# MLP rows of batches 4 and 5 turned by VectorE and SBUF transfers instead of TensorE, in a PixArt block on one Trainium2 core

## The chip, the cores and the metric

The kernel runs on one core of one Trainium2 chip. The core has a TensorE for matrix products (PE in the profile), a VectorE (DVE), a ScalarE (ACT), a GpSimd (POOL) and a SyncE (SP, which here only issues transfers). Each engine works through its own queue of instructions in order and waits on semaphores that the others set. All compute engines read and write an on-chip memory, the SBUF; matrix products end in a second one, the PSUM. The metric is the device time of one execution in microseconds (us). Before the change the median of three runs is 738.39 us (736.37, 740.21 and 738.39).

## The reference

One transformer block over 16 batches of 256 rows of 256 features, all float32: modulated self-attention, cross-attention to a context, and a modulated MLP. The change touches the MLP and the passage from attention to it.

```python
shift_a, scale_a, gate_a, shift_m, scale_m, gate_m = jnp.split(silu(c) @ W_mod + b_mod, 6, axis=-1)
...
x = x + c_attn_out                                   # end of cross-attention
x_norm2 = modulate(_ln(x), shift_m, scale_m)         # t * (1 + scale) + shift, per batch
h = gelu(x_norm2 @ W_mlp1 + b_mlp1)                  # 256 -> 1024
h = h @ W_mlp2 + b_mlp2                              # 1024 -> 256
x = x + gate_m[:, None] * h
```

## The kernel before, in words

Attention comes first. Thirty-two units (16 of self-attention, 16 of cross-attention) run in eight beats each; a plan says which pieces stand in each beat. The result of a batch's cross-attention, `t_c`, goes to DRAM (`x2d`). In the last units, words of a table named `TW` are dealt into the beats: `u0` to `u7` load the MLP weights, `h..` and `l..` split each weight into a high part and the rest (a product of float32 rows is made of three products of such parts, `mm3`), `x2` loads the rows of batch 2, `b2` adds the constant `cb` to them. A letter at the end names the engine: `d` VectorE, `p` or none GpSimd.

The MLP of a batch `b` is a chain of steps, each on its engine:

- `x`: load the rows from `x2d` (SP). `b`: add `cb` (GpSimd). `s`: statistics (VectorE: BN_STATS, BN_AGGR). `p`: the power that gives one over the deviation (GpSimd, `rs_m`). `a`: normalise (VectorE, `xn_m`).
- The rows must then stand with features on partitions. `mlp_T` (L833) has TensorE turn them (four transposes into `psT_m`), and VectorE and ScalarE scale, shift and split them into `hi` and `lo`. These two parts live in old weight tiles: `wkch` and `wkcl` for even batches, `wqch` and `wqcl` for odd ones.
- `mlp_turn` (L857) does it without TensorE: VectorE turns blocks of 32 by 32 (`z`), and four SBUF transfers issued by SP move the blocks to their partitions (`yT`). `mlp_turned` (L870) then scales and shifts on VectorE (two `z<-yT`), copies `hi` and subtracts to get `lo`. The rows of a turned batch come out in another order, and the GELU's writing puts it right by its access pattern (L931), at the cost of no further instruction.
- `F` j: first product, quarter j % 4 of batch j // 4, twelve TensorE products into `ph`. `G` j: two GELUs on ScalarE (`hf` in float32, `hh` rounded), then `hl` = `hf` - `hh` on GpSimd, written hl(j) below. `S` j: the twelve second products, which read `hh` and `hl`, into `st` (even batches) or `s` (odd ones). After a batch's last `S`, VectorE multiplies by the gate (`mt`) and adds the residual (`y`), and SP stores. `r` prepares that residual (`xmg`), `g` loads the gates (`gm`).

`TURN` (L855) says from which batch on the turned path is taken: 6 before. The passage from attention to MLP is written out as a string of words, `BE`; it reaches to the middle of batch 3 (F13 and S10). From then on a loop deals the rest. In it, one step is one quarter j; the loop issues G of j+1, F of j+2, S of j-1, and at fixed quarters the steps of the batches ahead:

```python
by_dma = [d if d < B and d >= TURN else None for d in range(b + 1, b + 4)]
by_pe = b + 2 if b + 2 < TURN else None
```

Batches in `by_dma` are loaded, biased and measured three batches ahead, and normalised and turned two ahead; the one in `by_pe` is prepared two ahead and turned by TensorE one ahead. Program order on every engine is the order in which these words are issued; nothing reorders them. A tile with a fixed number of buffers holds its next writer back until the last reader of the oldest buffer is done; `hh` and `hl` have three buffers each, so the GELU of j into `hh` waits for S of j-3.

Of the kernel before, what the change touches and what calls it, by code (L numbers as in the profile page):

```python
# [16 lines left out]
P = 128  # L17
# [4 lines left out]
def pixart_block(  # L22
# [85 lines left out]
    brow = const.tile([32, P], F32, name="brow")  # L108
# [151 lines left out]
    wm = []  # L260
# [9 lines left out]
    gm = []  # L270
# [19 lines left out]
    def layernorm(src, name):  # L290
# [542 lines left out]
    def mlp_T(b):  # L833
# [9 lines left out]
        for f in range(KC):  # L843
            DVE.tensor_scalar(y[:, f], pst[:, f * N:(f + 1) * N], sc1[:, 1, f, b:b + 1],
                              cpT[:, 6 + f, b:b + 1], ALU.mult, ALU.add)
        if b in E_['DV']:
            DVE.tensor_copy(hi, y)
# [4 lines left out]
        DVE.tensor_tensor(lo, y, hi, ALU.subtract)  # L852
        m.xT = (hi, lo)

    TURN = 6  # L855

    def mlp_turn(b):  # L857

# [23 lines left out]
    NCH = NF // 2  # L882

    def mlp_first(b, c):

        ph = ps_gen(f"ph_{b}_{c}", LONG).rearrange("p (j n) -> p j n", j=2)
        for j in range(2):
            mm3(ph[:, j], W1, 2 * c + j, M[b].xT)
        M[b].h[c] = ph
# [27 lines left out]
    def mlp_gelu(b, c):  # L917
# [6 lines left out]
        for dst in (hf, hh):  # L924
# [13 lines left out]
    def mlp_second(b, c):  # L938
# [15 lines left out]
        if done and b < B - 1:  # L954
            for t in range(NT):
# [7 lines left out]
    wf = {}  # L963

    steps = {"x": mlp_load, "b": mlp_bias, "s": mlp_stats, "p": lambda b: M[b].ln.pow(), "a": mlp_apply,
             "r": mlp_residual, "g": mlp_gates, "T": mlp_T, "F": lambda j: mlp_first(j // NCH, j % NCH),
             "G": lambda j: mlp_gelu(j // NCH, j % NCH), "S": lambda j: mlp_second(j // NCH, j % NCH)}

    def tail_word(w):
# [26 lines left out]
    u0, u1 = units[:2]  # L996
# [4 lines left out]
    u2 = units[2]  # L1001
# [42 lines left out]
    u3 = units[3]  # L1044
# [182 lines left out]
    last, o, q = units[-1], units[-1].post, units[-2].post  # L1227
# [97 lines left out]
```

## Time and profile before

| | |
|---|---|
| median of three runs | 738.39 us (736.37 to 740.21) |
| the profiled execution: its time | 737.4 us |
| its span, first to last instruction | 735.6 us |
| TensorE busy | 728.9 us (99%) |
| VectorE busy | 584.8 us (79%) |
| ScalarE busy | 555.5 us (76%) |
| GpSimd busy | 546.3 us (74%) |
| granted TensorE clock | 0.999 |

A row of a timeline gives the start in us from the span's beginning, the duration, the engine, the line, the operation, what is written and from what, its size, how many instructions were merged (their common span is the duration), and in brackets the idle time ahead of it with what ended that. Every operation goes through one recording helper, so all rows carry line 51; they are told apart by their tiles. TensorE products are pipelined: each lasts 0.28 us, but they start 0.12 us apart. In a row of waits stand the time waited in all, how often, and the longest.

### The profile page before, as it was taken

The page shows a single profiled execution, that of the slowest core. Times are in us where ns is not written, and L with a number is a line of the kernel's source. Part 1 is how long each engine was busy: PE and PEld are TensorE (multiplying, and loading weights), DVE is VectorE, ACT ScalarE, POOL GpSimd, SP SyncE. Part 2 cuts the span into 40 slices and gives each one's busy share as a digit, 9 for nine tenths or more (in the row PEclk, how much of TensorE's full clock was granted, in tenths as well). Part 3 has the DMA queues.
Part 4 walks back from the last instruction along what each step waited for, and adds up shares of the span by engine and source line. Part 5 has one row for each costly group of instructions (what it writes and reads, how often), then busy time and mean ns, then how long its engine had stood idle before and what let it go on. Part 6 is the DMA issues. An engine that isn't in the chain of part 4 may idle for free.

```text
span 735.6 us, 25307 instructions
## 1 busy us (share of the span) xinstructions
PE 728.9 (99%) x10112; PEld 644.8 (88%) x10112; DVE 584.8 (79%) x1217; ACT 555.5 (76%) x959; POOL 546.3 (74%) x571
## 2 busy tenths in 40 slices
PE   9999999999999999999999999999999999999997
PEld 9878888888888888888888888888889999999997
DVE  4788898989888888988888989888735577687772
ACT  3268898888888888888888888899887655555553
POOL 6777688869687786968778798788657766767753
PEclk9999999999999999999999999999999999999999
DMA  6754454543545454454545555455312323323331
GB/s 190 205 166 142 125 142 134 141 122 101 155 114 155 125 144 137 107 152 112 160 126 139 143 156 146 126 151 140 96 60 58 102 61 98 98 90 102 87 77 38
DMA packets 94825, 90.60 MB, mean 123 GB/s; under 512 B 9266, under 2 KB 90452, under 8 KB 94708
## 3 DMA queue, kind: packets, MB, share of 16 engines
q1 hardware_dynamic: 94244, 88.20, 42.8%
q8 instruction: 80, 1.31, 0.8%
q0 software_dynamic: 192, 0.52, 0.3%
q14 instruction: 37, 0.30, 0.1%
q10 hardware_dynamic: 272, 0.26, 0.1%
HBM read 26.97 MB, written 8.46 MB: 48 GB/s over the span
## 4 chain that ended last, share of the span: by engine, by line
PE 93%; DVE 3%; POOL 2%; issue 1%; ACT 1%; DMA 1%; SPq 0%; POOLq 0%; ACTq 0%
PE s L51 18%; PE o L51 16%; PE st L51 16%; PE ph L51 10%; PE ps_q L51 5%; PE ps_qc L51 4%; PE ps_v_c L51 3%; PE ps_kc L51 3%; PE ps_P_s L51 3%; PE ps_k L51 2%; PE ps_v_s L51 2%; PE ps_P_c L51 2%; DVE mx L51 1%; PE psT_q L51 1%; PE ps_h L51 1%; PE psA_s L51 1%
## 5 line engine op out<-in xcount | busy, mean ns | idle before, releaser
L51 DVE TENSOR_REDUCE mx<-s 128x2 f32<-128x512 f32 x504 | 324.8, 684 | 64.4 <-PE s L51 57.7
L51 ACT ACTIVATE pt<-st 128x1024 f32<-128x1024 f32 x252 | 258.9, 1027 | 16.4 <-PE st L51 10.4
L51 PE MATMUL s<-big 63*128 63x256 f32 (+1 forms) x1024 | 184.0, 297 | 0.2
L51 PEld LDWEIGHTS s<-big 63*128 63x128 f32 (+1 forms) x1024 | 133.4, 186 | 18.7 <-DVE l_kc L51 6.6
L51 PE MATMUL st<-big 64*128 64x256 f32 (+1 forms) x1024 | 134.6, 298 | 0.5 <-ACT pt L51 0.2
L51 POOL TENSOR_TENSOR hl<-hf,hh 128x512 fp32r<-128x512 f32 x64 | 87.0, 1361 | 52.9 <-ACT hh L51 52.8
L51 PE MATMUL o<-pt,v 128*32 128x256 f32 x2048 | 123.8, 382 | 0.0
L51 PEld LDWEIGHTS st<-big 64*128 64x128 f32 (+1 forms) x1024 | 96.3, 186 | 16.1 <-issue 13.1
L51 PEld LDWEIGHTS o<-pt,v 128*32 128x32 f32 x2048 | 60.1, 110 | 41.4
L51 ACT ACTIVATE hf<-ph,bT 128x256 f32<-128x256 f32 x114 | 47.8, 471 | 33.1 <-PE ph L51 33.0
L51 ACT ACTIVATE hh<-ph,bT 128x256 fp32r<-128x256 f32 x114 | 47.9, 472 | 28.0 <-PE s L51 14.4
L51 ACT COPY oT<-o 128x512 f32<-128x512 f32 x63 | 36.9, 586 | 33.1 <-PE o L51 33.1
L51 PE MATMUL st<-big,hh 128*128 128x256 f32 x256 | 46.7, 282 | 0.0
L51 PE MATMUL s<-big,hh 128*128 128x256 f32 x256 | 46.7, 281 | 0.0
L51 PE MATMUL ph<-wkch,wself 128*128 128x256 f32 x224 | 44.4, 282 | 0.0
L51 PE MATMUL ph<-wqch,wself 128*128 128x256 f32 x224 | 44.3, 282 | 0.0
L51 PE MATMUL ps_k<-xTh_s,wself 64*128 64x256 f32 (+1 forms) x232 | 43.6, 294 | 0.0
L51 POOL TENSOR_SCALAR xn_c<-c,mv_c,rs_c 128x256 f32<-128x256 f32 x32 | 39.0, 1227 | 1.7
L51 PE MATMUL ps_q<-xTh_s,wself 64*128 64x256 f32 (+1 forms) x240 | 39.7, 282 | 0.0
L51 PE MATMUL ps_P_s<-wself,xTh_as 64*128 64x256 f32 x256 | 39.1, 282 | 0.0
L51 PEld LDWEIGHTS s<-big,hh 128*128 128x128 f32 x256 | 39.0, 189 | 0.0
L51 PEld LDWEIGHTS st<-big,hh 128*128 128x128 f32 x256 | 39.0, 189 | 0.0
(250 smaller groups left out, 2500.4 us busy)
## 6 DMA issues: line engine op xcount, KB each, us to landing
big<-h_kc SPq DMA_DIRECT2D x64, 128.0 KB
big<-h_qc SPq DMA_DIRECT2D x64, 128.0 KB
big<-h_k SPq DMA_DIRECT2D x62, 128.0 KB
big<-h_q SPq DMA_DIRECT2D x62, 128.0 KB
big<-l_k SPq DMA_DIRECT2D x32, 128.0 KB
big<-l_q SPq DMA_DIRECT2D x32, 128.0 KB
g<-gd SPq DMA_DIRECT2D x16, 256.0 KB
c<-in_ctx_dram SPq DMA_DIRECT2D x16, 256.0 KB
```

Of the source, the lines that this page charges most:

```text
L51: i = f(*a, **k)
```

## The change

Three edits. `TURN` goes from 6 to 4, so batches 4 and 5 take the turned path. A new word `W` (`mlp_turn`) lets the string `BE` turn batch 4, which the loop comes too late to do, and the word `T` picks the path by batch. And the words of `TW` and `BE` are dealt anew; below, the entries that differ.

```diff
-    'TW': (23, 7): 'u1', (28, 0): 'l2 h0p u5', (28, 7): 'u4 u6', (29, 2): 'l1',
-          (30, 1): 'u7 h6d h7p', (30, 3): 'h4p', (31, 2): 'l5d x2', (31, 4): 'l7', (31, 7): 'b2'
+    'TW': (24, 4): 'u1', (28, 0): 'u5 l2 h0p', (28, 7): 'u4 u6 l1',
+          (30, 1): 'u7 h6d', (30, 3): 'h4p h7p', (31, 2): 'x2', (31, 3): 'l5d', (31, 4): 'l7 b2'
...
-    'BE': 'G0 av P g0 A1 G1 G2 N1 F7 g1 S0 PF s2 G3 aT aL p2 a2 G4 x3 b3 S1 S2 T2 C r0 G5 S3 G6 S4 s3 CF x4
-           F8 g2 G7 S5 F9 p3 S6 G8 a3 r1 G9 F10 G10 T3 g3 b4 S7 s4 F11 S8 S9 F12 G11 p4 a4 F13 r2 S10 G12 x5'
+    'BE': 'g0 G0 av P A1 G1 G2 N1 F7 g1 S0 PF s2 G3 aT aL x3 p2 a2 G4 b3 S1 S2 T2 C G5 r0 S3 G6 S4 s3 CF x4
+           F8 G7 g2 S5 F9 p3 S6 G8 a3 r1 G9 F10 G10 T3 S7 g3 b4 s4 F11 S8 x5 F12 G11 p4 a4 F13 S9 W4 r2 S10 G12 b5 s5'
...
-    TURN = 6
+    TURN = 4
...
-             ... "T": mlp_T,
+             ... "T": lambda b: (mlp_turned if b >= TURN else mlp_T)(b), "W": mlp_turn,
```

TensorE loses the turns of batches 4 and 5. This is the place in front of F14 (`ph_2` of batch 3), before, with four transposes of batch 4 between the last products of S10 and F14:

```order
L51 MATMUL st<-big_77,hh_2_12554 128x256 x2
L51 MATMUL st<-big_77,hl_2_12555 128x256
L51 MATMUL psT_m_12708<-ident,xn_m_12660 128x128 x4
L51 MATMUL ph_2_12721<-wqch,wself 128x256
L51 MATMUL ph_2_12721<-wqcl,wself 128x256
```

After the change F14 follows S10 directly there, the same is so at batch 5's turn in front of F18, and S9 stands behind F12 and F13 instead of ahead of them.

VectorE, from the statistics of batch 4 to the end of its rows, before (`xTf_m` is the scaled row from `psT_m`; ScalarE writes `wkch`):

```order
L51 BN_STATS st_m_12593<-x_4_12455 128x6 x2
L51 BN_AGGR mv_m_12596<-st_m_12593 128x2 x2
L51 TENSOR_SCALAR xn_m_12660<-x_4_12455,mv_m_12596,rs_m_12599 128x256 x2
L51 TENSOR_TENSOR xmg_12676<-x_2_12076,gm_12470 128x512
L51 TENSOR_SCALAR xTf_m_12713<-psT_m_12708,sc_103,cpT 128x256 x2
L51 TENSOR_TENSOR wkcl<-xTf_m_12713,wkch 128x512
L51 TENSOR_TENSOR mt_12734<-st,gm_12470 128x256 x2
L51 TENSOR_TENSOR y_12735<-xmg_12676,mt_12734 128x512
L51 BN_STATS st_m_12788<-x_5_12698 128x6 x2
L51 BN_AGGR mv_m_12791<-st_m_12788 128x2 x2
L51 TENSOR_SCALAR xn_m_12864<-x_5_12698,mv_m_12791,rs_m_12794 128x256 x2
```

The same place after the change, up to the turn of batch 5:

```order
L51 TENSOR_SCALAR xn_m_12650<-x_4_12455,mv_m_12596,rs_m_12599 128x256 x2
L51 STREAM_TRANSPOSE z_12678<-xn_m_12650 128x2x4x32 x2
L51 TENSOR_TENSOR xmg_12686<-x_2_12075,gm_12478 128x512
L51 BN_STATS st_m_12709<-x_5_12625 128x6 x2
L51 BN_AGGR mv_m_12712<-st_m_12709 128x2 x2
L51 TENSOR_SCALAR z_12678<-yT_12679,sc_103,cpT 128x4x64 x2
L51 COPY wkch<-z_12678 128x512
L51 TENSOR_TENSOR wkcl<-z_12678,wkch 128x512
L51 TENSOR_TENSOR mt_12745<-st,gm_12478 128x256 x2
L51 TENSOR_TENSOR y_12746<-xmg_12686,mt_12745 128x512
L51 TENSOR_SCALAR xn_m_12796<-x_5_12625,mv_m_12712,rs_m_12715 128x256 x2
L51 STREAM_TRANSPOSE z_12799<-xn_m_12796 128x2x4x32 x2
```

The turn of batch 4 stands behind its xn, the statistics of batch 5 have moved ahead of the rows of batch 4, and the copy into `wkch` is VectorE's own.

GpSimd at the same time, from the power of batch 4 on, before (`hl_0` is hl(12), `hl_1` hl(13) and so on; the small TENSOR_SCALAR and the TENSOR_TENSOR with `mhalf` are a power):

```order
L51 TENSOR_TENSOR rs_m_12599<-rs_m_12599,mhalf 128x2
L51 TENSOR_TENSOR hl_0_12692<-hf_0_12690,hh_0_12691 128x512
L51 TENSOR_TENSOR hl_1_12702<-hf_1_12700,hh_1_12701 128x512
L51 TENSOR_TENSOR x_5_12698<-x_5_12698,cb 128x512
L51 TENSOR_TENSOR hl_2_12755<-hf_2_12753,hh_2_12754 128x512
L51 TENSOR_TENSOR hl_3_12797<-hf_3_12795,hh_3_12796 128x512
L51 TENSOR_SCALAR rs_m_12794<-mv_m_12791 128x2
```

And after the change:

```order
L51 TENSOR_TENSOR rs_m_12599<-rs_m_12599,mhalf 128x2
L51 TENSOR_TENSOR hl_0_12702<-hf_0_12700,hh_0_12701 128x512
L51 TENSOR_TENSOR x_5_12625<-x_5_12625,cb 128x512
L51 TENSOR_SCALAR rs_m_12715<-mv_m_12712 128x2
L51 TENSOR_TENSOR rs_m_12715<-rs_m_12715,mhalf 128x2
L51 TENSOR_TENSOR hl_1_12720<-hf_1_12718,hh_1_12719 128x512
L51 TENSOR_TENSOR hl_2_12765<-hf_2_12763,hh_2_12764 128x512
L51 TENSOR_TENSOR hl_3_12811<-hf_3_12809,hh_3_12810 128x512
L51 TENSOR_TENSOR x_6_12730<-x_6_12730,cb 128x512
```

The bias add and the power of batch 5, which waits for VectorE's statistics, now stand ahead of hl(13), hl(14) and hl(15).

More of the change, by code (lines that the diff above doesn't have):

```diff
@@ new lines, in pixart_block @@
+    E_ = {'CUT': 8, 'LN': {'s': 'pool', 'c': 'pool', 'q': 'pool'}, 'ON': (1, 1, 1), 'L0': -16, 'L1': 1, 'S0': -7, 'A0': 0, 'T0': 1, 'S1': 5, 'A1': 7, 'L2': 9, 'T1': 9, 'S2': 32, 'AP': 23, 'DV': (0, 1), 'HP': (1, 0), 'BZ': {}, 'AV': {1: [(1, 2), (1, 3)], 9: [(0, 0), (0, 1)]}, 'AHEAD': (0, 0, 0, 0, 0, 2), 'TW': {(21, 6): 'cb', (23, 5): 'u0', (24, 4): 'u1', (25, 2): 'u2', (27, 3): 'u3', (27, 7): 'h2a', (28, 0): 'u5 l2 h0p', (28, 2): 'h1p', (28, 4): 'h3p', (28, 7): 'u4 u6 l1', (29, 0): 'l3d', (29, 1): 'l0', (29, 7): 'h5p', (30, 1): 'u7 h6d', (30, 3): 'h4p h7p', (31, 1): 'l4 l6d', (31, 2): 'x2', (31, 3): 'l5d', (31, 4): 'l7 b2'}, 'BE': 'g0 G0 av P A1 G1 G2 N1 F7 g1 S0 PF s2 G3 aT aL x3 p2 a2 G4 b3 S1 S2 T2 C G5 r0 S3 G6 S4 s3 CF x4 F8 G7 g2 S5 F9 p3 S6 G8 a3 r1 G9 F10 G10 T3 S7 g3 b4 s4 F11 S8 x5 F12 G11 p4 a4 F13 S9 W4 r2 S10 G12 b5 s5', 'XP': 1, 'IL': 1, 'MF': 0, 'SH': 4, 'RAMP': 1, 'HA': 1, 'MP': 16, 'W': (7, 1, 0, 0), 'PRE': 'load z0kp silu b12 turn brow L0a z0qp L0b b4 L0d T0t hik scale lok sc1 lg L1a b5 T0h L1b T0l ld2 one0 shift b3 K0a bk hiq lc L1d lp L2a K0m loq K0h T1t K0y0p T1h K0l K0x0 bq hiv K0l0 T1l z1qp K0x1 K0l1 Q0a Q0m K1a K0y1p lov Q0h Q0l Q0x1 K1b Q0l0 bv z1kp V0a Q0l1 Q0x0 Q1a Q1b L2b Q1y0 K1x0 V0b K1l b9 Q0y0p Q0y1p Q1l', 'SL': {(-1, 0): 'L2c ld3 K1l0 K1y1', (-1, 1): 'Q1l0 T2t Q1y1 V1a T2h Q1x0 K1l1 K1x1 T2p', (-1, 2): 'wm V1b Q1x1 z2kp vone', (-1, 3): 'ga K1y0', (-1, 4): 'pb M0 Q1l1 ld4 gs L3a', (-1, 5): 'L3b L3p one1', (-1, 6): 'one2 K2a L3c K2m', (-1, 7): 'z2qp mods cb', (0, 0): 'gm lx sp0', (0, 2): 'sp1 sc2', (0, 3): 'sp3', (0, 6): 'sp2', (1, 4): 'sp4'}}
@@ L965, in pixart_block @@
     steps = {"x": mlp_load, "b": mlp_bias, "s": mlp_stats, "p": lambda b: M[b].ln.pow(), "a": mlp_apply,
-             "r": mlp_residual, "g": mlp_gates, "T": mlp_T, "F": lambda j: mlp_first(j // NCH, j % NCH),
+             "r": mlp_residual, "g": mlp_gates, "T": lambda b: (mlp_turned if b >= TURN else mlp_T)(b), "W": mlp_turn, "F": lambda j: mlp_first(j // NCH, j % NCH),
              "G": lambda j: mlp_gelu(j // NCH, j % NCH), "S": lambda j: mlp_second(j // NCH, j % NCH)}
```

1 line of the change is left out of this document (removed).

## The prediction

> **What bounds the kernel.** I read the page first (busy shares, then the chain that ended last), then TensorE's waits from 520 us on, where every moved step lies.
>
> ```profile
> PE 728.9 (99%) x10112; PEld 644.8 (88%) x10112; DVE 584.8 (79%) x1217; ACT 555.5 (76%) x959; POOL 546.3 (74%) x571
> PE 93%; DVE 3%; POOL 2%; issue 1%; ACT 1%; DMA 1%; SPq 0%; POOLq 0%; ACTq 0%
> ```
>
> ```profile
> PE psT_m L51 <- DVE xn_m L51: 0.8, 2, 0.4
> PE ps_P_c L51 <- POOL xTl_ac L51: 0.2, 1, 0.2
> ```
>
> TensorE (PE) carries the chain, and from 520 us to the end it waited 1.0 us in all. So the change can gain its removed TensorE work and part of 1.0 us; it can lose without limit if TensorE starts to wait for rows. The question is when the rows of batches 4 and 5 are ready. F16 is the first product of batch 4, F20 of batch 5.
>
> ```profile
> 578.48 0.40 PE L51 MATMUL st<-big,hh 128*128 128x256 f32 x2
> 579.90 0.28 PE L51 MATMUL ph<-wqch,wself 128*128 128x256 f32 x1
> 582.76 0.40 PE L51 MATMUL st<-big,hh 128*128 128x256 f32 x2
> 584.18 0.60 PE L51 MATMUL psT_m<-ident,xn_m 128*128 128x128 f32 x4
> 584.53 0.37 PE L51 MATMUL ph<-wqch,wself 128*128 128x256 f32 x1
> 586.05 0.40 PE L51 MATMUL st<-big,hh 128*128 128x256 f32 x2
> 590.29 0.28 PE L51 MATMUL ph<-wkch,wself 128*128 128x256 f32 x1
> 595.96 0.27 PE L51 MATMUL psT_m<-ident,xn_m 128*128 128x128 f32 x1
> 596.86 0.37 PE L51 MATMUL ph<-wkch,wself 128*128 128x256 f32 x1
> 613.95 0.28 PE L51 MATMUL ph<-wkch,wself 128*128 128x256 f32 x1
> 625.29 0.28 PE L51 MATMUL ph<-wqch,wself 128*128 128x256 f32 x1
> ```
>
> These rows are TensorE before: S9, F12, S10, the turn of batch 4, F14, S11, F16, the turn of batch 5, F18, F24, F28. A group of 12 products takes 1.42 us (578.48 to 579.90), a batch of eight groups 11.34 (613.95 to 625.29).
>
> **Removed.** The turn of batch 4 is 0.35 us (584.18 to 584.53), and the group behind it takes 1.52 instead of 1.42 (584.53 to 586.05): 0.45. The turn of batch 5, with its wait for xn, is 0.90 (595.96 to 596.86). Sum: **-1.35 us**. ScalarE's four evacuations go too; it is not on the chain.
>
> **Words dealt anew.** Between attention and MLP the weight words move by a beat or a few on GpSimd, VectorE and SP (one W1 subtraction, a W2 copy, a bias add, a W1 load), and TensorE's order there is unchanged. Their cover is the slack that TensorE's waits show: one wait for GpSimd, 0.2 us. Bounds: -0.2 if that wait goes, +1.3 if a subtraction (1.3 us, as hl below) is passed on to TensorE. I take 0, nearest to the wait row. S9 behind F13 moves F12 from 579.90 to 578.48; I take 0, since TensorE does the same groups, with 0.1 (one product) as the bound if the low rows of batch 3 are not quite there. It holds back the second GELU of F12, hh, whose buffer S9 frees: that counts below.
>
> **Added: the turned path, from batches it already serves.** VectorE (DVE) of batch 6 and after:
>
> ```profile
> 582.53 0.73 DVE L51 TENSOR_SCALAR xn_m<-x,mv_m,rs_m 128x256 f32<-128x256 f32 x2 [1.41 <-POOL rs_m L51]
> 603.92 1.17 DVE L51 STREAM_TRANSPOSE z<-xn_m 128x256 f32<-128x256 f32 x2
> 609.37 1.74 DVE L51 TENSOR_SCALAR z<-yT,sc,cpT 128x256 f32<-128x256 f32 x2 [1.50 <-DMA yT<-z]
> 611.21 0.43 DVE L51 CAST wkch<-z 128x512 fp32r<-128x512 f32 x1
> 611.68 0.69 DVE L51 TENSOR_TENSOR wkcl<-z,wkch 128x512 fp32r<-128x512 f32 x1
> 612.28 0.75 DVE L51 TENSOR_TENSOR mt<-st,gm 128x256 f32<-128x256 f32 x2
> 613.07 1.00 DVE L51 TENSOR_TENSOR y<-xmg,mt 128x512 f32<-128x512 f32 x1
> 618.03 0.75 DVE L51 BATCH_NORM_STATS2 st_m<-x 128x6 f32<-128x256 f32 x2 [1.18 <-POOL x L51]
> 618.71 0.30 DVE L51 BATCH_NORM_AGGREGATE mv_m<-st_m 128x2 f32<-128x6 f32 x2
> 620.81 1.45 DVE L51 CAST wqch<-z 128x512 fp32r<-128x512 f32 x1
> 632.37 1.41 DVE L51 TENSOR_SCALAR z<-yT,sc,cpT 128x256 f32<-128x256 f32 x2 [2.02 <-DMA yT<-z]
> 710.38 0.73 DVE L51 TENSOR_SCALAR z<-yT,sc,cpT 128x256 f32<-128x256 f32 x2 [2.85 <-DMA yT<-z]
> ```
>
> SP's issues of the four transfers of a batch:
>
> ```profile
> 605.11 2.58 SPq L51 DMA_DIRECT2D yT<-z  x4
> 627.12 2.49 SPq L51 DMA_DIRECT2D yT<-z  x4
> 706.22 2.49 SPq L51 DMA_DIRECT2D yT<-z  x4
> ```
>
> From the first transfer's issue to VectorE's use are 4.26 us for the first of ten batches, 4.16 for the last, 5.25 for the slowest (627.12 to 632.37). I take 4.16. One loop joins the batches on VectorE: rows ready, mt, y, xn, z, transfers, scale and shift, copy, subtract. It closed in 10.6 us here (612.37 to 622.98, where the subtraction behind 620.81's copy ended by the same 0.69): less than TensorE's 11.34, but not by much.
>
> GpSimd (POOL) and VectorE hold each other up; one row of VectorE, seven of GpSimd, and one of ScalarE (ACT), which sets when GpSimd's hl can start:
>
> ```profile
> 560.60 1.37 DVE L51 TENSOR_SCALAR xn_m<-x,mv_m,rs_m 128x256 f32<-128x256 f32 x1
> ```
>
> ```profile
> 560.39 1.43 POOL L51 TENSOR_TENSOR hl<-hf,hh 128x512 fp32r<-128x512 f32 x1 [0.15 <-ACT hh L51]
> 612.18 1.34 POOL L51 TENSOR_TENSOR hl<-hf,hh 128x512 fp32r<-128x512 f32 x1 [1.54 <-ACT hh L51]
> 615.01 1.29 POOL L51 TENSOR_TENSOR hl<-hf,hh 128x512 fp32r<-128x512 f32 x1 [1.49 <-ACT hh L51]
> 616.27 1.73 POOL L51 TENSOR_TENSOR x<-x,cb 128x512 f32<-128x512 f32 x1
> 617.96 1.30 POOL L51 TENSOR_TENSOR hl<-hf,hh 128x512 fp32r<-128x512 f32 x1
> 619.64 0.78 POOL L51 TENSOR_TENSOR rs_m<-rs_m,mhalf 128x2 f32<-128x2 f32 x1
> 620.68 1.29 POOL L51 TENSOR_TENSOR hl<-hf,hh 128x512 fp32r<-128x512 f32 x1 [0.26 <-ACT hh L51]
> 623.51 1.29 POOL L51 TENSOR_TENSOR hl<-hf,hh 128x512 fp32r<-128x512 f32 x1 [1.54 <-ACT hh L51]
> ```
>
> ```profile
> 614.10 0.84 ACT L51 ACTIVATE hh<-ph,bT 128x256 fp32r<-128x256 f32 x2 [0.52 <-PE s L51]
> ```
>
> The second xn of 560.60 ends at 561.97, 0.15 after GpSimd's hl (561.82), which had come between the two. The copy of 620.81 ends 0.29 after hl (621.97), the y of 613.07 0.55 after hl (613.52). So a VectorE operation from SBUF waits for the running GpSimd one, and a GpSimd operation already waiting goes before VectorE's next.
>
> **Batch 4.** xn keeps 582.53 to 583.26, z ends at 584.4, the transfers land 4.16 later: scale and shift start at 588.55. What does GpSimd do then? hh of F12 now waits for S9, which ends where S10 starts (582.76); as in the ScalarE row (614.10 behind 613.95) it runs 582.9 to 583.75, hl(12) until 585.1, xmg 0.55, the bias add of batch 5 until 586.85. Statistics and aggregation (0.75 and 0.30) end at 587.8, the power of batch 5 (1.1, the 619.64 row and the small add ahead of it) at 588.9. hl(13) and hl(14), whose inputs are ready at 585.2 and 588.0 (the end of S10 and of S11, plus 0.15 and 0.84 for hh), stand queued behind that power; hl(15) can start at 590.8. So scale and shift (2 x 0.36) just get in; then hl(13) to 590.45, copy 0.29, hl(14) to 591.9, subtract 0.55: rows ready at **592.45**. TensorE reaches F16 at 590.29 - 0.45 = 589.84 and needs the low rows one product (0.12) later: **+2.5 us**. Bounds: with transfers 0.2 us slower the second shift loses its place and the rows come at 593.85 (+3.9); at 5.25 us 595.3 (+5.3); with no hold-up 590.5 (+0.5). On SP the four issues (2.5 us) stand behind the gate load of batch 3 and the load of batch 5, both issued by 581.7, and ahead of the load of batch 6, which GpSimd wants only at 593.8; hidden. If the load of batch 5 lands after 585.1, power and hl(13) come later and the shift gains room, so it is no loss. S13, which needs hl(13) (590.45), comes after F16; hidden too.
>
> **Batch 5.** The same loop from 592.45: mt ends 593.2, hl(15) holds y until 594.2, the bias add of batch 6 holds xn until 595.9, z ends 597.0, landing 601.15. hl(17), behind the power of batch 6, runs until 601.6, hl(18) from 602.0 to 603.3: the copy ends 603.6, the subtraction 604.35. F20 would be at 592.35 + 11.34 = 603.7: **+0.6**.
>
> **Batches 6 to 14.** Now the loop starts about 2 us later against GpSimd's beat than before (rows ready 612.37 for 613.95, 1.6 ahead). Counted from a batch's first product that waited 0.6: hl runs 0.5 to 1.8 (615.01 less 613.95, less the wait), y ends 2.3, the bias add 3.5, xn 4.0, z 5.05, landing 9.25; xmg lost to hl pushes statistics, power and the next hl back to 8.0-9.25; the shift ends 9.75, hl of 623.51 (9.56) goes ahead to 11.0, copy 11.3, subtract 12.0. That is 12.0 against 11.34: late by 0.6 again. In the old position, 1.6 to 2.3 ahead, y and xn fall ahead of hl and the loop stays early. So lateness feeds itself: nine batches x 0.6 = **+5.4**. Batch 15 has no bias add ahead of it and recovers.
>
> Sum: -1.35 + 2.5 + 0.6 + 5.4 = **+7.1 us** on a profiled execution of 737.4 (span 735.6 and 1.8 around it), which stands 1.0 below the median 738.39. I forecast **745.5**.
>
> [...]
>
> **Rivals.** *One stall, loop recovers.* If the transfers land 0.2 us later, the rows come at 593.85; then hl(15) is over, y and xn lose less against TensorE's later clock, rows 5 are ready at 603.4 for F20 at 605.1, and nothing follows: -1.35 + 3.9 = +2.5, at most -1.35 + 5.3 = +4.0: 741 to 742.4. For it: the margin of the shift against hl(13) is 0.1 us, and one of the three quoted transfers was that slow. Against: the typical transfer is not.
>
> *VectorE wins its turns.* If copy and subtraction of batch 4 go ahead of the waiting hl, rows come at 588.55 + 0.74 + 0.05 + 0.43 + 0.05 + 0.69 = 590.5, F16 waits 0.5, the loop (10.6) falls back ahead: -1.35 + 0.5 = -0.85, 737.5, not slower. It decides from rows ready by about 591.3, where the stall equals the removed work. Against it is 560.60, where VectorE's second half lost.
>
> **How the numbers follow.** Self-feeding lateness 0.50 (743 to 749: per-batch lateness 0.4 to 0.9), one stall 0.30, VectorE wins 0.20. The range 738 to 751 takes in the one-stall times, the bound of 1.3 on the moved words and lateness of 0.9 per batch behind the late landing; it leaves out most of the last rival. About 0.5% (3.7 us) can be told from no change. The main case is slower but for 0.02; one stall splits 0.17 within, 0.13 slower; the last 0.13 within, 0.07 faster, by the scatter alone, since the trace holds only 2.4 us to gain. So faster 0.07, same 0.32, slower 0.61.
>
> **What would show it.** No turn of batches 4 and 5 on TensorE; a wait of F16 for VectorE's wkch or wkcl of 2 to 3 us near 590; then F24, F28 and on 11.9 apart instead of 11.34, each behind a wait for the low rows, with copy and subtraction stretched by hl. A single wait with 11.34 behind it proves the first rival; none above 0.6, the second. I am wrong if F16's wait falls elsewhere (an SP transfer, S13 for hl(13)).

## The result, and the profile after

The changed kernel takes 742.91 us (median of six runs, 742.42 to 745.05). The kernel before, run on the same chip, takes 737.97 (six runs, 736.37 to 740.21). The ratio is 1.007, with an interval from 1.005 to 1.009: slower by 5 us. The profiled execution of the changed kernel took 743.9 us with a span of 742.1, against 737.4 and 735.6 before; so the two profiled executions lie 6.5 us apart, the medians 4.9.

From the page of the changed kernel, the busy times and the shares of the chain that ended last:

```profile
PE 731.2 (99%) x10104; PEld 646.4 (87%) x10104; DVE 590.4 (80%) x1223; ACT 554.1 (75%) x955; POOL 545.9 (74%) x571
...
PE 91%; DVE 3%; POOL 2%; DMA 1%; issue 1%; ACT 1%; SPq 0%; POOLq 0%; DVEq 0%; ACTq 0%
```

TensorE has eight products fewer (the two turns), and yet is busy 2.3 us longer. Its waits from 520 us on:

```profile
PE ph L51 <- DVE wkch L51: 3.1, 1, 3.1
PE ph L51 <- DVE wkcl L51: 1.2, 1, 1.2
PE psT_m L51 <- DVE xn_m L51: 0.4, 1, 0.4
PE ps_P_c L51 <- POOL xTl_ac L51: 0.2, 1, 0.2
```

One wait for the high rows, one for the low rows, and no more in the eleven batches that follow. TensorE's timeline shows where they stand: F16 and its second product, then the first products of batches 5, 6 and 7 (F20, F24, F28).

```profile
593.60 0.35 PE L51 MATMUL ph<-wkch,wself 128*128 128x256 f32 x1 [3.14 <-DVE wkch L51]
595.18 0.58 PE L51 MATMUL ph<-wkcl,wself 128*128 128x256 f32 x1 [1.23 <-DVE wkcl L51]
...
609.13 0.28 PE L51 MATMUL ph<-wqch,wself 128*128 128x256 f32 x1
...
620.47 0.28 PE L51 MATMUL ph<-wkch,wself 128*128 128x256 f32 x1
...
631.80 0.28 PE L51 MATMUL ph<-wqch,wself 128*128 128x256 f32 x1
```

F24 and F28 come 11.34 and 11.33 us behind their forerunners, as before the change. Batch 4, from 593.60 to 609.13, took 15.53. Of the 4.19 us too much, 1.46 are the second wait; the rest has another cause. This is the view by stretches of the changed kernel. Behind a stretch stand its length and then, with the counts of instructions, the busy us of TensorE, of its weight loads, of VectorE, ScalarE and GpSimd; the last three columns are TensorE's granted clock, the DMA share and GB/s.

```profile
586.00:590.00 4.00, 4.00 (x36) 4.00 (x36) 1.08 (x5) 2.52 (x6) 2.83 (x4) 1.00 0.36 75
590.00:593.00 3.00, 0.46 (x4) 0.25 (x3) 2.76 (x3) 0.84 (x2) 3.00 (x3) 1.00 0.22 75
593.00:595.00 2.00, 0.35 (x1) 0.19 (x1) 1.97 (x2) 0.00 (x0) 1.58 (x2) 0.82 0.00 0
595.00:598.00 3.00, 2.82 (x13) 2.82 (x14) 2.96 (x8) 0.07 (x1) 0.00 (x0) 0.50 0.18 60
598.00:601.00 3.00, 3.00 (x16) 3.00 (x16) 1.69 (x6) 1.43 (x4) 0.00 (x0) 0.50 0.32 77
```

After the wait TensorE ran at a granted clock of 0.50 until 601: the last row counts 16 products in 3 us, where the stretch of 3 us from 601 on counts 27. The products start 0.213 us apart there in place of 0.118; some 28 of them, 0.095 us slower each, make 2.6 us.

VectorE made the rows of batch 4 (the first four rows) and of batch 5 (the last three):

```profile
582.90 0.74 DVE L51 TENSOR_SCALAR xn_m<-x,mv_m,rs_m 128x256 f32<-128x256 f32 x2 [1.41 <-POOL rs_m L51]
...
590.14 1.92 DVE L51 TENSOR_SCALAR z<-yT,sc,cpT 128x256 f32<-128x256 f32 x2 [1.86 <-DMA yT<-z]
592.16 1.30 DVE L51 CAST wkch<-z 128x512 fp32r<-128x512 f32 x1
593.49 1.64 DVE L51 TENSOR_TENSOR wkcl<-z,wkch 128x512 fp32r<-128x512 f32 x1
...
602.36 0.74 DVE L51 TENSOR_SCALAR z<-yT,sc,cpT 128x256 f32<-128x256 f32 x2 [2.67 <-DMA yT<-z]
603.20 0.43 DVE L51 CAST wqch<-z 128x512 fp32r<-128x512 f32 x1
603.66 0.69 DVE L51 TENSOR_TENSOR wqcl<-z,wqch 128x512 fp32r<-128x512 f32 x1
```

GpSimd beside it, the power of batch 5, then the residues hl(13) to hl(15) without a gap, then the bias add of batch 6:

```profile
588.66 0.71 POOL L51 TENSOR_TENSOR rs_m<-rs_m,mhalf 128x2 f32<-128x2 f32 x1
589.34 3.83 POOL L51 TENSOR_TENSOR hl<-hf,hh 128x512 fp32r<-128x512 f32 x3
593.13 1.44 POOL L51 TENSOR_TENSOR x<-x,cb 128x512 f32<-128x512 f32 x1
```

And SP's issues of the transfers of batches 4 and 5:

```profile
584.74 3.66 SPq L51 DMA_DIRECT2D yT<-z  x4
...
598.30 2.50 SPq L51 DMA_DIRECT2D yT<-z  x4
```

The transfers of batch 4 were in use 5.40 us after their first issue (584.74 to 590.14), those of batch 5 after 4.06. Scale and shift came when three residues were queued on GpSimd, and all three of VectorE's operations on the rows took 2.4 to 3 times as long as for batch 5. The rows were ready at 595.13. TensorE's last product before the wait began at 590.18, so F16 was due at 590.3 and its second product, the first that needs the low rows, at 590.4.

The sum for the span: -1.35 (turns gone) + 4.8 (second product of batch 4, 590.4 to 595.18) + 2.6 (half clock) + 0.35 (F12 began at 578.84, not 578.48) + 0.1 (F12 and F13 took 2.95 us together, 2.86 before) = +6.5; measured 742.1 - 735.6 = +6.5. The 0.35 is no effect of the change: TensorE was already 0.3 us later at 65 us, long ahead of the first moved word, and the kernel before with another order in its loop (experiment 11), which is the same program up to the loop, began F12 0.40 later than the kernel before.

### The profile page after: what moved, and what is told of

It is laid out like the page before. It is cut to its first block, busy times and chain, and to the rows that moved or that the text cites. A ratio compares the mean times of both kernels' runs of the same rounds, so it can differ in the third digit from the quotient of the medians.

```text
span 742.1 us, 25306 instructions
## 1 busy us (share of the span) xinstructions
PE 731.2 (99%) x10104; PEld 646.4 (87%) x10104; DVE 590.4 (80%) x1223; ACT 554.1 (75%) x955; POOL 545.9 (74%) x571
## 3 DMA queue, kind: packets, MB, share of 16 engines
q8 instruction: 80, 1.31, 0.8%
## 4 chain that ended last, share of the span: by engine, by line
PE 91%; DVE 3%; POOL 2%; DMA 1%; issue 1%; ACT 1%; SPq 0%; POOLq 0%; DVEq 0%; ACTq 0%
PE s L51 18%; PE o L51 16%; PE st L51 15%; PE ph L51 10%; PE ps_q L51 5%; PE ps_qc L51 4%; PE ps_kc L51 4%; PE ps_v_c L51 3%; PE ps_P_s L51 3%; PE ps_k L51 2%; PE ps_v_s L51 2%; PE ps_P_c L51 2%; DVE mx L51 1%; PE psT_q L51 1%; POOL hl L51 1%
## 5 line engine op out<-in xcount | busy, mean ns | idle before, releaser
L51 POOL TENSOR_TENSOR hl<-hf,hh 128x512 fp32r<-128x512 f32 x64 | 85.4, 1340 | 61.2 <-ACT hh L51 61.2
L51 PEld LDWEIGHTS ph<-wkch,wself 128*128 128x128 f32 x224 | 37.5, 195 | 3.3 <-issue 3.3
```

What stands on the lines that cost most here:

```text
L51: i = f(*a, **k)
```

## The experiments

Each ratio is to the kernel before, run again at the same time on the same chip (medians of 737.23, 737.51, 737.06 and 737.12 us). All compute the full output; two add work that is never read, which is said there.

### 1. The words alone

Two edits of the changed kernel: no batch earlier turned, all else as dealt anew.

```diff
-    TURN = 4
+    TURN = 6
-    'BE': '... F13 S9 W4 r2 S10 G12 b5 s5'
+    'BE': '... F13 S9 r2 S10 G12'
```

> Only the words dealt anew, with TensorE still turning batches 4 and 5 (no turn of batch 4 by VectorE, batch 5 prepared by the loop as before). If the whole loss comes from the late rows of batch 4, this is as fast as before: 0 us, within 0.5 us, with no wait of F16 above 0.5 us and the clock at 1.00 throughout. If the moved words cost the time, it is 1 to 5 us slower than before, with TensorE's offset building up ahead of F12.

Measured: 737.46 us, ratio 1.0007 (0.9993 to 1.0021). The new deal of the words costs nothing and gains nothing; the loss comes from the turns.

### 2. Only batch 5 turned earlier

```diff
-    TURN = 4
+    TURN = 5
-    'BE': '... F13 S9 W4 r2 S10 G12 b5 s5'
+    'BE': '... F13 S9 r2 S10 G12 b5 s5'
```

> Batch 5 takes the turned path, batch 4 stays on TensorE. If the loss belongs to batch 4's start alone, the 0.9 us of batch 5's turn are gained and nothing is lost: 0.5 to 1 us faster than before, no wait at F20, clock 1.00. If a loop that starts in the middle is late whichever batch begins it, F20 waits 1 to 5 us and the run is 0 to 5 us slower than before.

Measured: 746.87 us, ratio 1.0115 (1.0088 to 1.0143): worse than turning both. TensorE's first products of batches 5, 7 and 9 in this kernel:

```profile
603.96 0.36 PE L51 MATMUL ph<-wqch,wself 128*128 128x256 f32 x1 [0.77 <-DVE wqch L51]
...
628.51 0.36 PE L51 MATMUL ph<-wqch,wself 128*128 128x256 f32 x1 [0.51 <-DVE wqch L51]
...
653.06 0.35 PE L51 MATMUL ph<-wqch,wself 128*128 128x256 f32 x1 [0.50 <-DVE wqch L51]
```

Two batches take 24.55 us in place of 22.67 (11.96 and 12.59 in turn, to the end of the loop), at a clock of 0.999. VectorE from the end of batch 8's rows to the end of batch 9's shows why it goes on:

```profile
640.31 0.69 DVE L51 TENSOR_TENSOR wkcl<-z,wkch 128x512 fp32r<-128x512 f32 x1
640.92 0.75 DVE L51 TENSOR_TENSOR mt<-st,gm 128x256 f32<-128x256 f32 x2
...
643.30 1.71 DVE L51 TENSOR_SCALAR xn_m<-x,mv_m,rs_m 128x256 f32<-128x256 f32 x2
644.93 1.15 DVE L51 STREAM_TRANSPOSE z<-xn_m 128x256 f32<-128x256 f32 x2
...
651.09 1.29 DVE L51 TENSOR_SCALAR z<-yT,sc,cpT 128x256 f32<-128x256 f32 x2 [3.36 <-DMA yT<-z]
652.49 0.43 DVE L51 CAST wqch<-z 128x512 fp32r<-128x512 f32 x1
652.95 0.69 DVE L51 TENSOR_TENSOR wqcl<-z,wqch 128x512 fp32r<-128x512 f32 x1
```

The rows of batch 8 end at 641.00, those of batch 9 at 653.64: 12.64 us round the loop that the prediction names, more than TensorE's 11.34. The xn took 1.71 us in place of 0.73, since GpSimd's bias add, 1.74 us from 642.79, ran beside it. So the lateness that feeds itself exists; it stands in this kernel, and not in the changed one. Over two batches it is 1.88 us (24.55 less 22.67), 0.9 a batch, where the prediction had 0.6. One of the six runs took 740.73: the loop can recover.

### 3. Power of batch 5 behind the two residues

The residues are hl(13) and hl(14).

```diff
-        if c == 0 and by_dma[1]:
+        if c == 0 and by_dma[1] and b > 3:
             M[by_dma[1]].ln.pow()
...
         if c == 1:
             if by_dma[1]:
+                if b == 3:
+                    M[5].ln.pow()
                 mlp_apply(by_dma[1])
```

> The change with one edit: the power of batch 5 stands behind hl(13) and hl(14) on GpSimd, not ahead of them. If the queue behind that power is what holds VectorE up, the copy of batch 4 is no longer stretched, the rows come at about 592.2 to 593.2 instead of 595.1 and F16 waits 1.8 to 2.8 us instead of 4.4 to 4.8. If the half clock needs the long wait, it is gone too and the run is 4 to 5 us faster than the change; if any wait of 2 us brings it, 2 us faster. If GpSimd is not the cause, nothing moves: F16 still waits over 4 us.

Measured: 744.96 us, ratio 1.008 (1.0053 to 1.0108), but the ten runs lie in two groups, four at 738.2 to 739.6 and six at 744.9 to 746.1. The profiled one is of the first group. Its two waits ahead of batch 4:

```profile
590.43 0.36 PE L51 MATMUL ph<-wkch,wself 128*128 128x256 f32 x1 [1.07 <-DVE wkch L51]
...
592.12 0.58 PE L51 MATMUL ph<-wkcl,wself 128*128 128x256 f32 x1 [1.33 <-DVE wkcl L51]
```

2.4 us of waiting, 2.0 less than in the changed kernel, so the power ahead of the residues cost about that. Behind it this run recovered. That the six at 745 are runs with the late loop is likely from their time, but none of them was profiled. Four of these six had a mean granted clock of 1.000, so no half clock; of the four faster ones three had 0.995 to 0.998 and one 1.000. Whether the half clock, which holds TensorE back by another 1.5 us or so (an estimate: 16 products in 3.41 us, at 0.213 us in place of 0.118), helps the loop to recover at this size of stall was not tested. The transfers of batch 4 were as late as before, 5.41 us.

### 4. Earlier loads

The loads of x for batch 5 and of the gates of batch 3 about 10 us earlier, out of the way of batch 4's transfers.

```diff
-    'BE': '... CF x4 F8 G7 g2 S5 ... S7 g3 b4 s4 F11 S8 x5 F12 ...'
+    'BE': '... CF x4 x5 F8 G7 g2 g3 S5 ... S7 b4 s4 F11 S8 F12 ...'
```

> The change with one edit: the load of batch 5 and the gates of batch 3 are issued some 10 us earlier, so that SP's queue is empty ahead of the four transfers of batch 4. If those two loads slowed the transfers, issue takes 2.5 us instead of 3.7 and the rows land 4.2 us after the first issue instead of 5.4; scale and shift just get in ahead of hl(13), rows at about 592.7, F16 waits about 2.3 us. Then the loop may stay late, 0.6 us per batch, as forecast as the likeliest; if it recovers, the run is 2.5 to 5 us faster than the change. If the transfers were slow for another reason, landing stays above 5 us and the run is as the change.

Measured: 742.63 us, ratio 1.0073 (1.0057 to 1.0089), the same as the changed kernel. The transfers landed after 4.99 us, still 0.8 late, and the waits were 3.13 and 1.03. The two loads cost the transfers at most 0.4 us; the rest of the lateness has another cause.

### What held them up: a table from all traces

The view of the DMA queues shows a second kind of traffic in the 2 us in which batch 4's transfers run. From the changed kernel, stretch 584 to 586:

```profile
q1 hardware_dynamic: 261, 0.26, 37.3%
q8 instruction: 1, 0.02, 4.2%
```

By the kind that the view gives, this is a load of instructions: one packet of 16 KB, whose time is 1.3 us (4.2% of 16 engines for 2 us). It is TensorE's code, to judge by the count: queue q8 has 80 such packets in the run, 1.31 MB, and TensorE has 10,104 products and as many weight loads, 253 a packet. Between the loads at 490.8 and 726.4, which are 19 loads apart, TensorE began 4,865 instructions (semaphore instructions included): 256 a load on average, 221 to 298 from one load to the next. The loads also keep step with TensorE: 14.6 us apart around 590 before (584.35 and 598.96), 21.0 in the changed kernel (585.38 and 606.35), where TensorE waited and then ran slowly. In the fourteen profiled kernels of this study VectorE waited 121 times for a batch's four transfers. Time from the first issue to use:

| load of TensorE's code begins | cases | us |
|---|---|---|
| within 0 to 3.3 us of the first issue | 34 | 4.46 to 5.83 |
| not in that time | 82 | 4.05 to 4.34, but for two of 4.58 and 4.61 |
| another engine's code load in that time | 5 | 4.06 to 4.93 |

Each of the 34 sets of four that met such a load was late, by 0.3 to 1.7 us against the prediction's 4.16. How a load makes them late is not shown, since the trace does not name the DMA engines; that it makes them late is tested in experiments 7 and 8, which move it.

### 5. TensorE kept busy through the wait

Forty products on zeros, whose result is never read, stand ahead of the first product of batch 4.

```diff
         if i + 2 < len(chunks):
+            if i + 2 == 16:
+                busy(20, ps_gen("ps_warm", SHORT))
             mlp_first(*chunks[i + 2])
```

> The changed kernel with 40 products on zeros (their result is never read) put on TensorE right ahead of the first product of batch 4; at 0.116 us each (18 of them take 2.1 us at the start of the kernel) they fill 4.65 us, from 590.4 to 595.0, about as long as TensorE waits there for the rows of batch 4 in the changed kernel (3.14 + 1.23 us, until 595.18). If the half clock that follows that wait in the changed kernel (granted clock 0.50 from 595 to 601, products 0.21 us apart for some 27 products) comes from TensorE having stood still, the clock stays at 1.00, batch 5 starts at about 606.5 in place of 609.13, and the time is 2.6 us below the changed kernel's: 740 to 741 against 742.9. If the half clock has another cause (a power limit, the place in the program), the time stays at 742 to 744 and the clock falls all the same. If what healed the later batches was the slow stretch itself, the later batches wait as they do where only batch 5 was turned, and the time is 745 or more at a clock of 1.00.

Measured: 740.73 us, ratio 1.0044 (1.0028 to 1.0059), 2.2 below the changed kernel. The same stretches as above, in this kernel:

```profile
590.00:593.00 3.00, 3.00 (x29) 3.00 (x28) 2.90 (x3) 0.84 (x2) 3.00 (x4) 1.00 0.14 49
593.00:595.00 2.00, 1.85 (x16) 1.65 (x16) 1.97 (x3) 0.00 (x0) 1.21 (x1) 1.00 0.00 0
595.00:598.00 3.00, 3.00 (x27) 3.00 (x27) 2.96 (x8) 1.05 (x3) 0.00 (x0) 1.00 0.26 87
598.00:601.00 3.00, 3.00 (x28) 3.00 (x27) 1.32 (x5) 1.84 (x6) 2.08 (x3) 1.00 0.32 68
```

The clock stays at 1.00 and 27 products go in 3 us: standing still was the cause of the half clock. One of the eight runs took 743.53 at a mean clock of 0.993, so the cure did not hold in every run. The later batches came in time here too (the low rows of batch 5 were 1.2 us ahead, 4.9 in the changed kernel), so after a stall of this size the loop recovers without the slow stretch behind it.

### 6. Batch 4's turn earlier

Apply and turn of batch 4 some 2 us earlier, with both edits of experiments 3 and 4, and 16 of 18 filling products at 22 us left out (`b` with a number in the list `PRE`: TensorE works on zeros while it would wait), to move TensorE's code loads (left out of experiment 2's kernel, the same 16 moved one by 5.0 us, experiment 7).

```diff
-    'BE': '... F10 G10 T3 S7 g3 b4 s4 F11 S8 x5 F12 G11 p4 a4 F13 S9 W4 r2 ...'
+    'BE': '... F10 b4 G10 T3 s4 p4 a4 W4 S7 F11 S8 F12 G11 F13 S9 r2 ...'
-    'PRE': '... V0b K1l b9 Q0y0p ...'
+    'PRE': '... V0b K1l b1 Q0y0p ...'
```

> Everything that made batch 4 late is taken away together: the words of batch 4's normalisation and turn stand some 2 us earlier, both x loads earlier, the power of batch 5 behind the apply, and 16 of 18 filling products at the start of the kernel are left out, which moves TensorE's loads of its own instructions 32 instructions, some 1.8 us, later. Theory (batch 4's wait was lateness of 2.4 to 4.8 us and nothing else; turning two batches saves 1.35 us of TensorE): no wait at the first product of batch 4, or under 0.5 us, the later batches in time, 736 to 737, ratio 0.998 to 0.9995. Rival (the loop falls into the late order however batch 4 comes, as where only batch 5 was turned): F16 without a wait, but 0.5 to 1 us of waiting at each later batch, 743 to 747.

Measured: 744.8 us, ratio 1.0096 (1.0081 to 1.0112). The rival was right. TensorE's waits on the rows from 520 us on:

```profile
PE ph L51 <- DVE wkch L51: 2.2, 6, 0.6
PE ph L51 <- DVE wkcl L51: 1.7, 6, 0.3
PE ph L51 <- DVE wqcl L51: 1.1, 4, 0.3
```

The wait ahead of batch 4 fell to 0.64 + 0.28 us, and in place of two waits, 4.4 us together, there are sixteen small ones: batches 11.96 and 12.1 to 12.6 us apart, as in experiment 2. With most of the stall cured, this kernel fell into the state that the prediction had taken for the likeliest.

### 7. The code load moved away from batch 5's transfers

Experiment 2's kernel with 16 filling products and their weight loads, 32 instructions, taken out at 22 us.

```diff
-    'PRE': '... V0b K1l b9 Q0y0p ...'
+    'PRE': '... V0b K1l b1 Q0y0p ...'
```

> The kernel in which batch 5 is the first turned one (746.87) with one edit far away: 16 of the 18 filling products at 22 us left out, with their weight loads 32 instructions of TensorE fewer. In that kernel a 16 KB load of instructions stood at 3.0 us behind the first issue of batch 5's four transfers, which landed 5.34 us after it; 32 instructions later, at 256 instructions per 14.3 us, it comes 1.8 us later, behind their end. Theory (the load of instructions holds up one of the DMA engines and makes the transfers late, and that lateness starts the late loop): the transfers land 4.1 to 4.3 us after their first issue, no wait at the first product of batch 5, and the kernel stands at the words-only kernel's 737.46 less 0.9 for the products of one batch's turn: 736 to 738. Half-way theory (the load sets the landing but the late order of the loop comes from elsewhere): landing 4.1 to 4.3, and still 745 to 748. Rival (the transfers are slow because they are the first ones, or because of other loads): landing 5.0 to 5.4 and 745 to 748.

Measured: 746.22 us, ratio 1.0121 (1.0101 to 1.0141). The transfers of batch 5 landed after 4.23 us (597.88 to 602.11), not 5.34, with no load beside them, and the loop was late all the same. The load began at 605.28, 5.0 us later than in experiment 2 (600.28) and not the expected 1.8: the loads come 256 instructions apart on average, but not evenly (221 to 298 in the changed kernel). That is the half-way theory: the load sets the landing, but does not bring about the late loop.

### 8. The code load moved away from batch 4's transfers

The changed kernel with 32 more filling products at 22 us, whose result is never read.

```diff
-    'PRE': '... V0b K1l b9 Q0y0p ...'
+    'PRE': '... V0b K1l b9 b16 Q0y0p ...'
```

> The changed kernel with 32 more filling products at 22 us, where 18 stand already: at 0.116 us each they put off all that follows by up to 3.7 us, and they bring the 16 KB loads of TensorE's instructions 64 instructions, some 3.6 us, earlier against the work. In the changed kernel such a load stood 0.5 us behind the first issue of batch 4's transfers (584.74), which landed after 5.40 us. Theory (the load makes the transfers late): they land in 4.1 to 4.3 us, the scale and shift of batch 4 get to VectorE ahead of the three residues, and TensorE's waits ahead of batch 4 fall from 4.4 us to 1.0 to 2.9; time 742.9 + 3.7 - 1.5 to 3.4, to which comes up to 2 us of the half clock gone: 741 to 745. Rival (first transfers, x loads or the slow issue itself): landing 5.0 to 5.4, waits of 4.0 to 4.8 us, 745.5 to 747.

Measured: 744.34 us, ratio 1.0124 (1.0084 to 1.0164; two of the six runs took 751). SP's and VectorE's rows for batch 4 in this kernel, where all stands 2.8 us later:

```profile
587.54 2.58 SPq L51 DMA_DIRECT2D yT<-z  x4
```

```profile
591.88 0.73 DVE L51 TENSOR_SCALAR z<-yT,sc,cpT 128x256 f32<-128x256 f32 x2 [0.44 <-DMA yT<-z]
```

The load came at 582 to 584, ahead of the transfers. They landed after 4.34 us in place of 5.40, SP's issue took 2.58 in place of 3.66, scale and shift took 0.73 in place of 1.92, and TensorE's waits ahead of batch 4 fell from 4.4 to 2.1 (0.92 for ScalarE's hh, 1.22 for the low rows). So some 2 us of the stall came from the load of instructions. The time did not fall, since the products added at 22 us cost 2.8. The profiled run recovered; the two at 751 were not profiled.

### 9 to 11. The rows ahead of the end of a batch

In the loop, normalisation and turn of the next batch but one now stand right behind the rows of the next batch, ahead of `mt` and `y`, 1.75 us, instead of behind them.

```diff
         if c == 0 and by_dma[2]:
             mlp_load(by_dma[2])
+        if c == 0 and by_dma[1]:
+            mlp_apply(by_dma[1])
+            mlp_turn(by_dma[1])
...
         if c == 1:
-            if by_dma[1]:
-                mlp_apply(by_dma[1])
-                mlp_turn(by_dma[1])
```

In experiment 2's kernel:

> The kernel in which batch 5 is the first turned one (746.87, its batches 11.96 and 12.59 us apart in turn) with the loop's words in another order: the normalisation and turn of the next batch but one stand right behind the rows of the next batch, ahead of the two products with the gates and the sum that ends a batch (1.75 us of VectorE). Theory (the lateness feeds itself round a closed way on VectorE: rows of one batch, end of a batch, normalisation, turn, transfers of 4.2 us, rows of the next batch; in the late state the rows come only 0.15 us ahead of TensorE): 1.75 us taken out of that way is more than the 0.62 to 1.25 us by which it is too long, so the batches come every 11.34 us, rows 1.5 us or more ahead, and the time is the words-only kernel's 737.46 less 0.9: 736 to 738. Rival (VectorE or GpSimd has too much to do in all, or the late state comes from the words ahead of the loop): still 12.2 us a batch, 745 to 748. Half of each: the late state lasts for some batches and heals, 738 to 743.

With batch 4's turn earlier (`BE` and `PRE` of experiment 6):

> Batch 4's turn some 2 us earlier and 16 filling products fewer, as in the run that had 744.8 (there 0.9 us of waiting ahead of batch 4 and then the late state of 11.96 and 12.3 to 12.6 us a batch), with the same new order in the loop (the power stays ahead of its apply, at the head of a batch). Theory: 0.3 to 1.2 us of waiting ahead of batch 4, then 11.34 us a batch; 738 less 1.35 less 0.3 for nothing else, and plus the wait: 736 to 738, within 0.3% of the kernel before on either side. Rival (the late state needs no closed way, or batch 4's own wait grows by the reorder): 741 or more.

In the kernel before:

> The kernel before (batch 6 the first turned one) with the new order in the loop and nothing else. Its batches come every 11.34 us with rows 1.7 to 3.0 us ahead, so both theories give no change: 737 to 738 (ratio 0.998 to 1.002), with rows some 3 us ahead or more by the theory of the closed way. If the runs of the kernel before that take 739 to 740 are runs in which something in the loop is late for some batches, they become rarer. Slower by more than 1 us would say that the order costs something by itself (the end of a batch put off by 1.9 us).

Measured: 737.72 us, ratio 1.0008 (0.9995 to 1.0021), where experiment 2 had 746.87; 737.97, ratio 1.0018 (1.0006 to 1.0029), where experiment 6 had 744.8; and 737.63, ratio 1.0002 (0.9991 to 1.0013), for the kernel before. In the second the wait ahead of batch 4 was more than expected, 1.15 + 1.22 us, with 3.3 us at half clock behind it: its transfers landed after 5.58 us, beside a code load. TensorE's waits from 520 us on in the first of the three:

```profile
PE ph L51 <- ACT hh L51: 1.0, 1, 1.0
PE psT_m L51 <- DVE xn_m L51: 0.4, 1, 0.4
PE ps_P_c L51 <- POOL xTl_ac L51: 0.2, 1, 0.2
```

None is for rows of a turned batch. Batches come every 11.34 us, with the high rows 5.09 us ahead from batch 9 on in all three kernels (5.4 to 5.7 for the last batch); before the change they were 2.3 to 4.3 ahead. VectorE's row no longer waits for the transfers:

```profile
632.74 1.11 DVE L51 TENSOR_SCALAR z<-yT,sc,cpT 128x256 f32<-128x256 f32 x2
```

So the closed way (rows of one batch, end of a batch, normalisation, turn, transfers, rows of the next) was the cause of the late loop: the one edit takes 1.75 us of VectorE's work off it. The xn still takes 1.71 us beside GpSimd (635.03, for one), so it is not that the edit took the hold-up away. In the kernel before, which was early, the same edit gave a longer lead and the same time.

### 12. What the earlier turn is worth

In experiment 9 TensorE still waited 1.0 us for hh: VectorE stood 3.2 us at the statistics of batch 5, for an x whose bias add was late, with batch 4's rows queued behind them. Here bias add, statistics and power of batch 5 come after the rows of batch 4.

```diff
-    'BE': '... F13 S9 r2 S10 G12 b5 s5'
+    'BE': '... F13 S9 r2 S10 G12'
...
-        if c == 0 and by_dma[1]:
+        if c == 0 and by_dma[1] and b > 3:
             M[by_dma[1]].ln.pow()
...
         if c == 0 and by_dma[1]:
+            if b == 3:
+                mlp_bias(5)
+                mlp_stats(5)
+                M[5].ln.pow()
             mlp_apply(by_dma[1])
```

> The kernel that turns from batch 5 on with the loop's new order (737.72), and one edit more: bias add, statistics and power of batch 5 stand behind the rows of batch 4 on VectorE, not ahead of them. In that kernel TensorE waited 1.0 us for ScalarE's hh ahead of batch 4: VectorE stood 3.2 us at the statistics of batch 5 (waiting for the bias add of a late x) with the rows of batch 4 queued behind. Theory (that queueing cost back what turning batch 5 saves): the wait of 1.0 us goes, no wait over 0.4 us is left on TensorE from batch 4 on, and the time is the words-only kernel's 737.46 less 0.9: 736 to 737, ratio 0.997 to 1.000. Rival (the wait on hh comes from ScalarE's own order): it stays, 737.4 to 738. Worse: the normalisation of batch 5 now waits on VectorE for its power with the end of batch 2 behind it, and batch 5's rows come late: 738 to 740.

Measured: 736.88 us, ratio 0.999 (0.9977 to 1.0003). The wait on hh is gone; 0.5 us of waiting for the rows of batch 5 is new. TensorE's waits there:

```profile
PE ph L51 <- DVE wqcl L51: 0.3, 1, 0.3
PE ph L51 <- DVE wqch L51: 0.2, 1, 0.2
```

With the wait on hh cured, turning one batch more is worth 0.9 us less 0.5 us, which these runs cannot tell from nothing.

## Why the prediction was right or wrong

- **Time, sign and range: right, but the time by luck.** 745.5 forecast, range 738 to 751, 742.91 measured, slower. The sum behind the 745.5 is not what happened.
- **Removed, -1.35: right as far as it can be seen**: it closes the sum of the span (+6.5). What the turn of batch 5 left to gain is bounded by experiment 12.
- **Words dealt anew, 0: right** (experiment 1, 1.0007). The bound of 0.1 for the low rows of batch 3 was reached (F12 and F13, 2.95 us for 2.86).
- **Batch 4, +2.5: mis-sized.** The failing step is "I take 4.16" for the transfers; they took 5.40. The prediction had the slow case among its rows (5.25, from 627.12, before) and its price (rows at 595.3; measured 595.13), but took the typical one without asking what made the slow one slow. In both it was a load of instructions, 2.9 us behind the first issue there and 0.6 here. The rest of the step held: hl(13) to hl(15) queued behind the power of batch 5, a shift that loses its place, a copy and a subtraction stretched by GpSimd (1.30 and 1.64). It was 4.8 in place of 2.5. Taken away singly, the load was worth 2.3 us of waiting (experiment 8) and the power 2.0 (experiment 3).
- **The half clock, +2.6: missing.** No step asked what TensorE does after a stall.
- **Batch 5, +0.6, and the self-feeding lateness, +5.4: wrong for the changed kernel**, as the first rival said: the loop recovered, since a stall of 4.8 us gave VectorE time to get ahead (rows of batch 5 at 604.35 for F20 at 609.13). The mechanism was right and its size near: experiments 2 and 6 show it for the batches from the sixth on, by 0.6 to 1.25 us each (0.9 on average in experiment 2), and experiments 9 and 10 take it away by shortening the closed way. The step that failed is the start, where the prediction let the loop be late after a stall of 2.5 us. With about 1 us of waiting the loop stays late (experiments 2 and 6; one run in six of experiment 2 did not), with 2.1 and 2.4 the runs split (two late in six of experiment 8, six in ten of experiment 3, to judge by their times), with 4.2 and 4.4 none was late (experiment 4, the changed kernel). In the profiled runs it goes by the low rows of batch 5: 1.2 to 4.9 us ahead where the loop recovered, 0.2 to 0.5 late where it did not. That a longer stall is what gives this lead is argued from these runs, which differ in other words too.
- **The first rival (741 to 742.4)** is what happened, but for the half clock: -1.35 + 4.8 = +3.5, as in experiment 5, which has 740.73. The time came near the forecast by luck, because errors had opposite signs: 6.0 too much for batch 5 and the loop, 5.3 too little for batch 4 (2.3), the half clock (2.6), the scatter ahead of F12 (0.35) and F12 and F13 (0.1).
- **The second rival** asked that copy and subtraction go ahead of a waiting residue. They did not: 1.30 and 1.64 us beside residues and bias add, in place of 0.43 and 0.69. So the prediction's reading of VectorE and GpSimd, that a waiting GpSimd operation goes first, held here.

## What to carry to other kernels

A step that moves from an engine on the chain to one beside it closes a way of its own: add up its whole length, hold-ups by other engines and transfers included, and compare it with the period of the chain (10.6 against 11.34 us before). Where the margin is below one hold-up (1.3 to 1.7 us of GpSimd here), put the work on that way first, ahead of what nobody waits for. A stall can cost more than itself (waits of 2.1 to 2.4 us brought 3.41 us at a clock of 0.50 here), but it can also hide a worse state, so curing the stall alone may gain nothing (744.8 for 742.9). And when a transfer is late for no reason in the program, look for loads of instructions in the DMA view (here 4.46 to 5.83 us from issue to use beside one of TensorE's, in 80 of 82 cases 4.05 to 4.34 without).

## What the runs showed of the hardware

- **After a stall TensorE's granted clock was 0.50, for 3.41 or 6.83 us.** Waits of 1.07 + 1.33, 1.15 + 1.22 and 0.92 + 1.22 us, each with one product between, brought 3.41 us of clock 0.50 (experiments 3, 10, 8); 3.14 + 1.23 and 3.13 + 1.03 brought 6.83 (the changed kernel, experiment 4); 0.64 + 0.28, and 0.98 alone, brought none (experiments 6, 9). Times between changes of the clock were whole multiples of 3.413 us: 2 and 41 in the changed kernel (down at 594.26, up at 601.09, down at 741.04), 162 between those at 38.90 and 591.85 of experiment 3, 199 between those at 57.38 and 736.63 of experiment 9. The 3.41 us ahead of a fall were not without work: TensorE was busy for 1.27, 1.50 and 1.56 us of them in experiments 3, 8 and 10. In experiments 6 and 9 the emptiest 3.41 us, counted in the same steps, had 2.77 and 2.66 us busy, and the clock stayed at 1.00.
- **Four SBUF transfers of 64 KB beside a load of TensorE's code were late**, by 0.3 to 1.7 us (in use after 4.46 to 5.83 us in 34 cases, 4.05 to 4.34 in 80 of the 82 without). The loads moved against the work when 32 TensorE instructions were left out 560 us earlier (from 600.28 to 605.28, experiment 7) or 64 added (from 0.6 us behind the transfers' first issue to ahead of it, experiment 8).
- **One program, two paces.** Experiment 3 ran at about 739 or 745 us by the run, experiment 8 at 744 or 751. What decides it in a given run was not found.
